# A selective-scan kernel: one 1024-column scan a state in two double-bank PSUM tiles, and all rows of C by DMA

## The chip, the cores and the metric

One core of a Trainium2 chip runs the whole program. Five engines work side by side, each with its own queue in order: TensorE (PE, with its weight loads PEld), VectorE (DVE), ScalarE (ACT), GpSimd (POOL) and SyncE (SP), which here only issues DMAs. The metric is the device time of one execution in microseconds. The time before is the median of three runs.

## The reference

The input x has 16 sequences of 256 steps and 256 features, with a condition vector for each sequence. Four blocks follow one another: a conditioned low-rank adapter, a bidirectional selective state-space layer (Mamba) with a gated MLP, an attention block with 16 heads of 64, and an attention block with 16 heads of 16. Nearly all the time goes into the scan of the second block. Cut to that:

```python
xz = h @ in_w;  xs, z = split(xz);  xs = silu(xs)
proj = xs @ xproj_w                      # 512 + 64 + 64 columns
dt = softplus(proj[..., :512] + dt_bias);  Bm, Cm = the next 64, the last 64
A = -exp(A_log)                          # 512 x 64
def step(hst, (dt_t, B_t, C_t, x_t)):
    hst = hst * exp(dt_t[:, :, None] * A) + (dt_t * x_t)[:, :, None] * B_t[:, None, :]
    y_t = einsum('bds,bs->bd', hst, C_t)
y = ys + xs * Dskip
return y * silu(z) @ out_w
```

It is done once forward in time and once on the sequence reversed, with weights of its own, and the two results are added into x through a gate. There are 64 states, 512 channels and 256 steps, in fp32.

## The kernel before, in words

Channels lie on partitions: 512 channels are 4 chunks (`IC`) of 128 partitions, each with 256 columns of time. A unit is one sequence in one direction; there are 32 units, `units[u] = (b, d)`, and each has 64 states (`NS`). The list `steps` holds all 2048 pairs of unit and state, and the main loop goes over it one state at a time. For a state the work runs through four engines:

- `drive(k)` on POOL (L931): h = dt*x times the row of B of this state, 128 x 1024. The rows of B come as broadcasts from DRAM, four states to a tile `bb` (`load_b`, L901). `drive` runs four states ahead of the scan.
- `decay(k)` on ACT (L946): exp(dt * A) for the state, one activation for each of the four chunks, into PSUM. The tiles `decays` hold half a state each (two chunks, 512 columns, one PSUM bank), and there are `ND` = 3 of them in rotation. Column 0 of each half chunk was set to zero once (L270), so that a scan over two chunks starts anew at the second; the activations write columns 1 to 255 alone. In the backward direction they read time backward.
- `scan(k)` on DVE (L974): two scans of 512 columns, each h = decay * h + input along time, in place in `h`. In the backward direction h is read and written from its end.
- The product with C, in place in `h`: for states with `s % 8` in 0, 2, 3, 5, 6 on DVE (L977), with C from a PSUM tile `cs`, for 1, 4, 7 on POOL (L981), with C from a DRAM broadcast `cb` that holds three rows for eight states (`load_c`, L907). `cs` is made by `spread` (L961): TensorE transposes a column of `cT`, repeated 128 times, into one of two halves of a PSUM bank. So 1280 states have a multiply on DVE and 768 on POOL.
- `add_up(k)` on PE (L992): eight transposes that add into `y` in PSUM, two states behind the scan. An `h` buffer comes free after it; there are 11 (`NH`).

`front(u)` prepares a unit (projections, softplus, the row matrices of B and C written to DRAM as `bd`), `back(u)` applies the output projection, and `rest(b)` runs the remaining layers of a sequence that is finished. Both are generators; the main loop takes a step or two of them for each state, so that their TensorE, ACT and DVE work lies between the scans. The order within an engine's queue is set by the framework's scheduler; what stands under `keep_in_program_order` (POOL's work) stays in the order of the source. After the loop the layers of the last sequence run alone in the tail, with the scan's PSUM tiles as additional banks (`alone`).

PSUM has eight banks: three for `decays`, one for `cs`, two for `y`, two for all other products.

Of the kernel before, what the change touches and what calls it, by code (L numbers as in the profile page):

```python
# [15 lines left out]
P = 128  # L16
# [6 lines left out]
NS = 64  # L23
EPS = 1e-5


# [28 lines left out]
def kernel(ctx: ExitStack, tc: tile.TileContext, a: dict, out: bass.AP):  # L55
# [68 lines left out]
    SG = 4  # L124
    ND = 3
    NH = 11
# [7 lines left out]
    ps_y = ctx.enter_context(tc.tile_pool(name="ps_y", bufs=1, space=PSUM))  # L134
    ps_c = ctx.enter_context(tc.tile_pool(name="ps_c", bufs=1, space=PSUM))
    ps_g = ctx.enter_context(tc.tile_pool(name="ps_g", bufs=2, space=PSUM))
# [119 lines left out]
    for d in ("fwd", "bwd"):  # L256
        an = res.tile([P, IC, NS], F32, name=f"a_neg_{d}")
        nc.sync.dma_start(an, a[f"L1_cond_{d}_A_log"].rearrange("(c p) s -> p c s", p=P))
        nc.scalar.activation(an, an, AF.Exp)
        nc.vector.tensor_scalar(an, an, -1.0, None, ALU.mult)  # L260
        a_neg.append(an)
        w_bc.append(res.tile([P, IC, 2 * NS], F32, name=f"w_bc_{d}"))
        nc.sync.dma_start(w_bc[-1], chunked(a[f"L1_cond_{d}_xproj_w"])[:, :, DI:])
        w_out.append(res.tile([P, IC, D], F32, name=f"w_out_{d}"))
        nc.sync.dma_start(w_out[-1], chunked(a[f"L1_cond_{d}_out_w"]))


    decays = [ps_y.tile([P, 2, T], F32, name=f"decay{j}") for j in range(ND)]
    for dc in decays:
        nc.vector.memset(dc[:, :, 0:1], 0.0)  # L270

# [101 lines left out]
    def front(u):  # L373
# [13 lines left out]
        w_in, w_dt = wfront.pop(u)  # L387
        xz = s2.tile([P, 2 * IC, T], F32, name="xz")
        for m in range(0, 2 * IC, 2):
            px = halves(bank1("pxz"))  # L390
            for j in range(2):
                for c in range(DC):
                    nc.tensor.matmul(  # L393
                        px[:, j], w_in[:, c, (m + j) * P : (m + j + 1) * P], hT[:, c],
                        start=(c == 0), stop=(c == DC - 1),
                    )
                yield
            nc.scalar.copy(xz[:, m : m + 2], px)
        nc.scalar.activation(xz, xz, AF.Silu)
        exp_table()  # L400
        yield
        pb = bank1("pbc")
        for c in range(IC):
            nc.tensor.matmul(pb[:, :T], w_bc[d][:, c], xz[:, c], start=(c == 0), stop=(c == IC - 1))
        bc = s1.tile([P, T], F32, name="bc", tag="uu")
# [3 lines left out]
        yield  # L409
        pt = bank1("pct")  # L410
        for t in range(NT):
            nc.tensor.transpose(pt[:, t * P : (t + 1) * P], bc[:, t * P : (t + 1) * P], ident)
        cT = s2.tile([P, NT, NS], F32, name="cT")
        nc.scalar.copy(cT, pt[:, :T].rearrange("p (t s) -> p t s", t=NT)[:, :, NS:])
        yield


        pr = s1.tile([P, IC, T], F32, name="pr")
        for m in range(0, IC, 2):
            pp = halves(bank1("pdt"))  # L420
            for j in range(2):
                for c in range(IC):
                    nc.tensor.matmul(  # L423
                        pp[:, j], w_dt[:, c, (m + j) * P : (m + j + 1) * P], xz[:, c],
                        start=(c == 0), stop=(c == IC - 1),
                    )
                yield
# [32 lines left out]
        yield  # L460
        tc.keep_in_program_order(nc.gpsimd.tensor_tensor(dtx, dt, xz[:, 0:IC], ALU.mult))  # L461
        st[u] = (xz, cT, bd, dt, dtx)
        yield

    def back(u, yg):
# [12 lines left out]
        for m in range(DC):  # L478
            xb = xs[b][:, m]
            nc.vector.scalar_tensor_tensor(  # L480
                xb, po[:, m], m_mamba[:, 4 + m, b : b + 1], xb, ALU.mult, ALU.add
            )
# [409 lines left out]

    bbs, cbs, ys, made, hs, skips = {}, {}, {}, {}, {}, {}
    cs = ps_c.tile([P, 2, T], F32, name="cs")
    steps = [(u, s) for u in range(len(units)) for s in range(NS)]
    turn = [0]

# [6 lines left out]
    def load_c(u, g):  # L904
        bd = st[u][2]
        cb = s3.tile([P, 3, T], F32, name="cb")
        nc.sync.dma_start(  # L907
            cb,
            bd[NS + 8 * g + 1 : NS + 8 * g + 8 : 3, :].partition_broadcast(P),
        )  # L910
        cbs[u, g] = cb

    def drive(k):
        u, s = steps[k]
        if s % SG == 0:
# [19 lines left out]
    def decay(k):  # L935
        u, s = steps[k]
        d = units[u][1]

        when = slice(1, T) if d == 0 else slice(T - 2, None, -1)
        made[k] = []  # L940
        for i in range(2):
            dc = decays[turn[0] % ND]
            turn[0] += 1
            for j in range(2):
                c = 2 * i + (j if d == 0 else 1 - j)
                nc.scalar.activation(  # L946
                    dc[:, j, 1:T], st[u][3][:, c, when], AF.Exp, scale=a_neg[d][:, c, s : s + 1]
                )
            made[k].append(dc)


    near = [k for k, (u, s) in enumerate(steps) if s % 8 in (0, 2, 3, 5, 6)]
    nth = {k: i for i, k in enumerate(near)}

    def spread(i):

        if i >= len(near):
            return
        u, s = steps[near[i]]
        for t in range(NT):  # L960
            nc.tensor.transpose(  # L961
                cs[:, i % 2, t * P : (t + 1) * P], st[u][1][:, t, s : s + 1].to_broadcast([P, P]), ident
            )

    def scan(k):
        u, s = steps[k]
        d = units[u][1]
        h = hs[k]
        for i, dc in enumerate(made.pop(k)):
            hv = h[:, 2 * i : 2 * i + 2].rearrange("p c t -> p (c t)")  # L970
            dv = dc.rearrange("p c t -> p (c t)")
            if d == 1:
                hv = hv[:, ::-1]
            nc.vector.tensor_tensor_scan(hv, dv, hv, 0.0, ALU.mult, ALU.add)  # L974
        if k in nth:
            c = cs[:, nth[k] % 2]
            nc.vector.tensor_tensor(h, h, c.unsqueeze(1).to_broadcast([P, IC, T]), ALU.mult)  # L977
        else:
            c = cbs[u, s // 8][:, (s % 8) // 3]
            tc.keep_in_program_order(  # L980
                nc.gpsimd.tensor_tensor(h, h, c.unsqueeze(1).to_broadcast([P, IC, T]), ALU.mult)  # L981
            )

    def add_up(k):
# [4 lines left out]
        for n, h in enumerate(([skips.pop(u)] if s == 0 else []) + [hs.pop(k)]):  # L989
            for t in range(NT):  # L990
                for c in range(IC):
# [5 lines left out]
                    )  # L997

# [142 lines left out]
    decay(0)  # L1141
    spread(0)
    spread(1)
    other = late()
    for k in range(len(steps) + BEHIND):
# [9 lines left out]
        if k >= BEHIND:  # L1155
            add_up(k - BEHIND)
        if k - 1 in nth:
            spread(nth[k - 1] + 2)
        if k >= BEHIND:
            u, s = steps[k - BEHIND]  # L1160
            if s == NS - 1:
# [5 lines left out]
                for i in range(2):  # L1167
                    py = halves(bank1("py"))
                    for j in range(2):
# [3 lines left out]
                    nc.vector.tensor_tensor(  # L1173
                        yg[:, 2 * i : 2 * i + 2], py, st[u][0][:, IC + 2 * i : IC + 2 * i + 2], ALU.mult
                    )
# [39 lines left out]
```

## Time and profile before

| what | value |
|---|---|
| median of three runs | 7624.67 us (7620.87 to 7626.77) |
| the profiled execution, first to last instruction (span) | 7616.3 us |
| median of the runs less this span | 8.4 us |
| mean granted TensorE clock | 0.932 |
| DMA, mean | 89 GB/s, 675.90 MB |

The profile is one execution of its own; its page gives the span, and no other time for it. For each group of instructions it gives the source line, engine, operation, the tiles written and read, shape, count, then busy time in us and the mean duration of one in ns, then the idle time of the engine just before these instructions, with what ended most of it. Durations of neighbours on one engine overlap at the ends, so that start-to-start distances are shorter than a row's mean. A wait row says which engine and line waited for which, with the sum, the number of times and the longest, in us. A timeline row gives the start, the length, the engine, the line and how many instructions were merged.

### The profile page before, as it was taken

How to read it: one execution, taken by the hardware profiler on the slowest of the kernel's cores; microseconds unless marked ns; L12 is line 12 of the kernel's file. 1: busy time of each engine (PE TensorE's matmuls, PEld its weight loads, DVE VectorE, ACT ScalarE, POOL GpSimd, SP SyncE). 2: the span in 40 equal slices, each digit the busy share in tenths (PEclk: the TensorE clock that was granted, in tenths of full speed). 3: DMA queues.
4: the chain of work that ended last, by engine and by line, in shares of the span. 5: the costliest groups of instructions: out<-in, count | busy, mean ns of one | idle time of the engine just before them, and what ended most of it. 6: DMA issues, size and time to landing. Idle time of an engine off the chain costs nothing.

```text
span 7616.3 us, 100847 instructions
## 1 busy us (share of the span) xinstructions
PE 6249.2 (82%) x35471; PEld 4952.4 (65%) x35471; DVE 6860.6 (90%) x6887; ACT 5431.2 (71%) x12141; POOL 6843.8 (90%) x2959
## 2 busy tenths in 40 slices
PE   7568888888888888888888888888888888888778
PEld 4456676666667666676666666666666766666655
DVE  3988999999999999999999999999999999999982
ACT  4567777777777777777777777777777777777753
POOL 3999999999999999999999999999999999999960
PEclk8679999999999999999999999999999999999999
DMA  4112232222322222232222223222232222322221
GB/s 166 54 65 92 89 102 76 87 92 88 103 85 93 80 91 95 92 103 73 88 92 91 100 86 98 78 92 93 87 106 79 94 84 89 101 91 89 73 68 49
DMA packets 331644, 675.90 MB, mean 89 GB/s; under 512 B 24724, under 2 KB 204032, under 8 KB 326784
## 3 DMA queue, kind: packets, MB, share of 16 engines
q1 hardware_dynamic: 331136, 669.44, 26.7%
q8 instruction: 280, 4.59, 0.2%
q14 instruction: 228, 1.87, 0.1%
HBM read 650.22 MB, written 10.75 MB: 87 GB/s over the span
## 4 chain that ended last, share of the span: by engine, by line
DVE 47%; POOL 15%; issue 14%; ACT 12%; PE 10%; DVEq 0%; POOLq 0%; ACTq 0%
DVE h L974 34%; POOL h L931 8%; DVE h L977 8%; ACT decay L946 5%; POOL h L981 5%; PE y L992 3%; DVE maxima L682 1%; ACT L155 1%; PE dense L500 1%; PE down L511 1%; PE bank L108 1%; PE po L605 1%; POOL uu L452 1%; POOL dt L458 1%; POOL dtx L461 1%
## 5 line engine op out<-in xcount | busy, mean ns | idle before, releaser
L974 DVE TENSOR_TENSOR_SCAN h<-decay,h 128x512 f32<-128x512 f32 x4096 | 4748.8, 1213 | 283.1 <-ACT decay L946 196.6
L931 POOL TENSOR_TENSOR h<-dtx,bb 128x1024 f32<-128x1024 f32 x2048 | 4793.5, 2367 | 129.2 <-PE y L992 128.4
L992 PE MATMUL y<-ident,h 128*128 128x128 f32 x16384 | 2385.3, 292 | 693.0 <-POOL h L981 639.1
L992 PEld LDWEIGHTS y<-ident,h 128*128 128x128 f32 x16384 | 2054.6, 151 | 1047.6 <-POOL h L981 733.1
L946 ACT ACTIVATE decay<-dt,a_neg_bwd 128x255 f32<-128x255 f32 x4096 | 1816.8, 471 | 759.9 <-DVE h L974 718.3
L946 ACT ACTIVATE decay<-dt,a_neg_fwd 128x255 f32<-128x255 f32 x4096 | 1824.6, 474 | 613.0 <-DVE h L974 571.6
L981 POOL TENSOR_TENSOR h<-h,cb 128x1024 f32<-128x1024 f32 x768 | 1813.2, 2361 | 289.8 <-DVE h L974 275.1
L977 DVE TENSOR_TENSOR h<-h,cs 128x1024 f32<-128x1024 f32 x1280 | 1533.5, 1215 | 66.2 <-PE cs L961 56.6
L961 PE MATMUL cs<-ident,cT 128*128 128x128 f32 x2560 | 521.6, 294 | 131.8 <-DVE h L977 130.3
L961 PEld LDWEIGHTS cs<-ident,cT 128*128 128x128 f32 x2560 | 331.4, 147 | 216.0 <-DVE h L977 192.0
L572 PE MATMUL sc<-k,q 64*128 64x256 f32 x960 | 293.4, 429 | 16.7 <-ACT ex L581 16.0
L393 PE MATMUL pxz<-hTm,w_in 128*128 128x256 f32 x1024 | 267.6, 388 | 15.9 <-DVE maxima L682 12.1
L679 PE MATMUL sc<-kd,qk 128*128 128x512 f32 x490 | 251.4, 614 | 33.5 <-DVE maxima L682 20.8
L700 PE MATMUL scT<-qk,kd 128*128 128x256 f32 x984 | 251.1, 386 | 28.7 <-DVE qk L691 23.2
L581 ACT ACTIVATE ex<-sc,nmax 128x256 f32<-128x256 f32 x480 | 222.7, 468 | 71.2 <-DVE nmax L577 68.5
L423 PE MATMUL pdt<-xz,w_dt 128*128 128x256 f32 x1024 | 247.3, 385 | 0.0
L572 PEld LDWEIGHTS sc<-k,q 64*128 64x128 f32 x960 | 172.6, 200 | 105.3 <-issue 34.2
L393 PEld LDWEIGHTS pxz<-hTm,w_in 128*128 128x128 f32 x1024 | 181.4, 194 | 53.1 <-DVE maxima L682 15.5
L700 PEld LDWEIGHTS scT<-qk,kd 128*128 128x128 f32 x984 | 175.5, 190 | 60.7 <-ACT pr L429 25.0
L577 DVE TENSOR_REDUCE nmax<-sc 128x2 f32<-128x512 f32 x240 | 163.9, 683 | 49.5 <-PE sc L572 48.8
L423 PEld LDWEIGHTS pdt<-xz,w_dt 128*128 128x128 f32 x1024 | 190.7, 194 | 22.2
L595 ACT COPY exT<-pt 128x512 f32<-128x512 f32 x240 | 140.0, 583 | 86.2 <-PE pt L591 84.0
(350 smaller groups left out, 7571.4 us busy)
## 6 DMA issues: line engine op xcount, KB each, us to landing
bb<-bd SPq DMA_DIRECT2D x512, 512.0 KB
cb<-bd SPq DMA_DIRECT2D x256, 384.0 KB
l2w<-in_L_cond_W_dram SPq DMA_DIRECT2D x32, 1024.0 KB
l3w<-in_L_cond_W_dram SPq DMA_DIRECT2D x32, 1024.0 KB
l1w<-in_L_cond_mlp_w_dram SPq DMA_DIRECT2D x48, 512.0 KB
w_in<-in_L_cond_fwd_in_w_dram SPq DMA_DIRECT2D x16, 1024.0 KB
w_dt<-_L_cond_fwd_xproj_w_dram SPq DMA_DIRECT2D x16, 1024.0 KB
w_in<-in_L_cond_bwd_in_w_dram SPq DMA_DIRECT2D x16, 1024.0 KB
```

What stands on the lines that cost most here:

```text
L393: nc.tensor.matmul(px[:, j], w_in[:, c, (m + j) * P : (m + j + 1) * P], hT[:, c], start=(c == 0), stop=(c == DC - 1),)
L423: nc.tensor.matmul(pp[:, j], w_dt[:, c, (m + j) * P : (m + j + 1) * P], xz[:, c], start=(c == 0), stop=(c == IC - 1),)
L572: nc.tensor.matmul(sc[:, t], q[base : base + 64, ch, t * P : (t + 1) * P], k[base : base + 64, ch], start=True, stop=True,)
L679: nc.tensor.matmul(sc, q[:, g, t * P : (t + 1) * P], kd[g % 2][:, 2 * i : 2 * i + 2], start=True, stop=True)
L700: nc.tensor.matmul(sc[:, kt], kd[g % 2][:, j, kt * P : (kt + 1) * P], q[:, g], start=True, stop=True)
L931: nc.gpsimd.tensor_tensor(h, st[u][4], bb.unsqueeze(1).to_broadcast([P, IC, T]), ALU.mult)
L946: nc.scalar.activation(dc[:, j, 1:T], st[u][3][:, c, when], AF.Exp, scale=a_neg[d][:, c, s : s + 1])
L961: nc.tensor.transpose(cs[:, i % 2, t * P : (t + 1) * P], st[u][1][:, t, s : s + 1].to_broadcast([P, P]), ident)
L974: nc.vector.tensor_tensor_scan(hv, dv, hv, 0.0, ALU.mult, ALU.add)
L977: nc.vector.tensor_tensor(h, h, c.unsqueeze(1).to_broadcast([P, IC, T]), ALU.mult)
L981: nc.gpsimd.tensor_tensor(h, h, c.unsqueeze(1).to_broadcast([P, IC, T]), ALU.mult)
L992: nc.tensor.matmul(ys[u][:, t, c * P : (c + 1) * P], h[:, c, t * P : (t + 1) * P], ident, start=(s == 0 and n == 0 and c == 0), stop=(s == ...
```

## The change: what it does

- `decays` becomes two tiles of a whole state each (four chunks, 1024 columns, two banks). The bank of `cs` goes.
- A state has one scan of 1024 columns. For the 1280 states with the product on DVE it writes in place into the decay tile in PSUM, and the multiply reads it there and writes `h`; for the others the scan writes `h`.
- The reset at the start of each chunk no longer comes from a zeroed column: after `front` has used dt, POOL sets its column 0 to 1e34 (`APART`), and A is kept at or below -1e-30, so that the decay there is exp of a very negative number, zero. The activations write all 256 columns.
- All rows of C come by DMA: `cb` holds four states, and one load is made for every four states. `spread`, `cT` and the two transposes that made it go.
- The backward unit is held in reversed time from the projections on: the copies out of PSUM in `front` reverse it, and `back` reverses the result when it is added. Scan and decays have no reversed form any more.
- `xz` becomes two tiles, `xv` (one buffer) and `zv` (two), each with a Silu of its own.

```diff
-    ND = 3
+    ND = 2
...
-        nc.vector.tensor_scalar(an, an, -1.0, None, ALU.mult)
+        nc.vector.tensor_scalar(an, an, -1.0, LEAST, ALU.mult, ALU.min)
...
-    decays = [ps_y.tile([P, 2, T], F32, name=f"decay{j}") for j in range(ND)]
-    for dc in decays:
-        nc.vector.memset(dc[:, :, 0:1], 0.0)
+    decays = [ps_y.tile([P, IC, T], F32, name=f"decay{j}") for j in range(ND)]
...
-            nc.scalar.copy(xz[:, m : m + 2], px)
-        nc.scalar.activation(xz, xz, AF.Silu)
+            to = (xv, zv)[m // IC][:, m % IC : m % IC + 2]
+            nc.scalar.copy(to, px[:, :, ::-1] if d else px)
+        for v in (xv, zv):
+            nc.scalar.activation(v, v, AF.Silu)
...
-        pt = bank1("pct")
-        for t in range(NT):
-            nc.tensor.transpose(pt[:, t * P : (t + 1) * P], bc[:, t * P : (t + 1) * P], ident)
-        cT = s2.tile([P, NT, NS], F32, name="cT")
-        nc.scalar.copy(cT, pt[:, :T].rearrange("p (t s) -> p t s", t=NT)[:, :, NS:])
...
-        tc.keep_in_program_order(nc.gpsimd.tensor_tensor(dtx, dt, xz[:, 0:IC], ALU.mult))
+        tc.keep_in_program_order(nc.gpsimd.tensor_tensor(dtx, dt, xv, ALU.mult))
+        tc.keep_in_program_order(nc.gpsimd.memset(dt[:, :, 0:1], APART))
...
-        cb = s3.tile([P, 3, T], F32, name="cb")
-        nc.sync.dma_start(
-            cb,
-            bd[NS + 8 * g + 1 : NS + 8 * g + 8 : 3, :].partition_broadcast(P),
-        )
+        cb = s3.tile([P, SG, T], F32, name="cb")
+        nc.sync.dma_start(cb, bd[NS + g * SG : NS + (g + 1) * SG, :].partition_broadcast(P))
...
-            if s % 8 == 0:
-                load_c(u, s // 8)
+            load_c(u, s // SG)
...
-        when = slice(1, T) if d == 0 else slice(T - 2, None, -1)
-        made[k] = []
-        for i in range(2):
-            dc = decays[turn[0] % ND]
-            turn[0] += 1
-            for j in range(2):
-                c = 2 * i + (j if d == 0 else 1 - j)
-                nc.scalar.activation(
-                    dc[:, j, 1:T], st[u][3][:, c, when], AF.Exp, scale=a_neg[d][:, c, s : s + 1]
-                )
-            made[k].append(dc)
+        dc = decays[k % ND]
+        for c in range(IC):
+            nc.scalar.activation(dc[:, c], st[u][3][:, c], AF.Exp, scale=a_neg[d][:, c, s : s + 1])
...
-        for i, dc in enumerate(made.pop(k)):
-            hv = h[:, 2 * i : 2 * i + 2].rearrange("p c t -> p (c t)")
-            dv = dc.rearrange("p c t -> p (c t)")
-            if d == 1:
-                hv = hv[:, ::-1]
-            nc.vector.tensor_tensor_scan(hv, dv, hv, 0.0, ALU.mult, ALU.add)
-        if k in nth:
-            c = cs[:, nth[k] % 2]
-            nc.vector.tensor_tensor(h, h, c.unsqueeze(1).to_broadcast([P, IC, T]), ALU.mult)
+        h, dc = hs[k], decays[k % ND]
+        c = cbs[u, s // SG][:, s % SG].unsqueeze(1).to_broadcast([P, IC, T])
+        if s % 8 in (0, 2, 3, 5, 6):
+            nc.vector.tensor_tensor_scan(flat(dc), flat(dc), flat(h), 0.0, ALU.mult, ALU.add)
+            nc.vector.tensor_tensor(h, dc, c, ALU.mult)
         else:
-            c = cbs[u, s // 8][:, (s % 8) // 3]
-            tc.keep_in_program_order(
-                nc.gpsimd.tensor_tensor(h, h, c.unsqueeze(1).to_broadcast([P, IC, T]), ALU.mult)
-            )
+            nc.vector.tensor_tensor_scan(flat(h), flat(dc), flat(h), 0.0, ALU.mult, ALU.add)
+            tc.keep_in_program_order(nc.gpsimd.tensor_tensor(h, h, c, ALU.mult))
...
-    alone += [None] + [t.rearrange("p c t -> p (c t)") for t in (decays[0], cs, decays[1])]
-    alone += [None, decays[2].rearrange("p c t -> p (c t)")]
+    for dc in decays:
+        alone += [None] + [flat(dc[:, i : i + 2]) for i in (0, 2)]
```

More of the change, by code (lines that the diff above doesn't have):

```diff
@@ L24 @@
 EPS = 1e-5
+APART, LEAST = 1e34, -1e-30
 COLUMNS = [
@@ L134 @@
     ps_y = ctx.enter_context(tc.tile_pool(name="ps_y", bufs=1, space=PSUM))
-    ps_c = ctx.enter_context(tc.tile_pool(name="ps_c", bufs=1, space=PSUM))
     ps_g = ctx.enter_context(tc.tile_pool(name="ps_g", bufs=2, space=PSUM))
@@ L387, in front @@
         w_in, w_dt = wfront.pop(u)
-        xz = s2.tile([P, 2 * IC, T], F32, name="xz")
+        xv = s1.tile([P, IC, T], F32, name="xv")
+        zv = s2.tile([P, IC, T], F32, name="zv")
         for m in range(0, 2 * IC, 2):
@@ L403, in front @@
         for c in range(IC):
-            nc.tensor.matmul(pb[:, :T], w_bc[d][:, c], xz[:, c], start=(c == 0), stop=(c == IC - 1))
+            nc.tensor.matmul(pb[:, :T], w_bc[d][:, c], xv[:, c], start=(c == 0), stop=(c == IC - 1))
         bc = s1.tile([P, T], F32, name="bc", tag="uu")
@@ L408, in front @@
         nc.sync.dma_start(bd, bc)
-        yield
-        pt = bank1("pct")
-        for t in range(NT):
-            nc.tensor.transpose(pt[:, t * P : (t + 1) * P], bc[:, t * P : (t + 1) * P], ident)
-        cT = s2.tile([P, NT, NS], F32, name="cT")
-        nc.scalar.copy(cT, pt[:, :T].rearrange("p (t s) -> p t s", t=NT)[:, :, NS:])
         yield
@@ L423, in front @@
                     nc.tensor.matmul(
-                        pp[:, j], w_dt[:, c, (m + j) * P : (m + j + 1) * P], xz[:, c],
+                        pp[:, j], w_dt[:, c, (m + j) * P : (m + j + 1) * P], xv[:, c],
                         start=(c == 0), stop=(c == IC - 1),
@@ L460, in front @@
         yield
-        tc.keep_in_program_order(nc.gpsimd.tensor_tensor(dtx, dt, xz[:, 0:IC], ALU.mult))
-        st[u] = (xz, cT, bd, dt, dtx)
+        tc.keep_in_program_order(nc.gpsimd.tensor_tensor(dtx, dt, xv, ALU.mult))
+        tc.keep_in_program_order(nc.gpsimd.memset(dt[:, :, 0:1], APART))
+        st[u] = (xv, zv, bd, dt, dtx)
         yield
@@ L480, in back @@
             nc.vector.scalar_tensor_tensor(
-                xb, po[:, m], m_mamba[:, 4 + m, b : b + 1], xb, ALU.mult, ALU.add
+                xb, po[:, m, ::-1] if d else po[:, m], m_mamba[:, 4 + m, b : b + 1], xb, ALU.mult, ALU.add
             )
@@ L890, in beside @@
             yield from front(following)
-    bbs, cbs, ys, made, hs, skips = {}, {}, {}, {}, {}, {}
-    cs = ps_c.tile([P, 2, T], F32, name="cs")
+    bbs, cbs, ys, hs, skips = {}, {}, {}, {}, {}
     steps = [(u, s) for u in range(len(units)) for s in range(NS)]
-    turn = [0]
     def load_b(u, g):
@@ L937, in decay, with flat @@
         d = units[u][1]
-        when = slice(1, T) if d == 0 else slice(T - 2, None, -1)
-        made[k] = []
-        for i in range(2):
-            dc = decays[turn[0] % ND]
-            turn[0] += 1
-            for j in range(2):
-                c = 2 * i + (j if d == 0 else 1 - j)
-                nc.scalar.activation(
-                    dc[:, j, 1:T], st[u][3][:, c, when], AF.Exp, scale=a_neg[d][:, c, s : s + 1]
-                )
-            made[k].append(dc)
[L952 to L962, printed above, removed]
-            )
+        dc = decays[k % ND]
+        for c in range(IC):
+            nc.scalar.activation(dc[:, c], st[u][3][:, c], AF.Exp, scale=a_neg[d][:, c, s : s + 1])
+    def flat(t):
+        return t.rearrange("p c t -> p (c t)")
     def scan(k):
         u, s = steps[k]
-        d = units[u][1]
-        h = hs[k]
-        for i, dc in enumerate(made.pop(k)):
-            hv = h[:, 2 * i : 2 * i + 2].rearrange("p c t -> p (c t)")
-            dv = dc.rearrange("p c t -> p (c t)")
-            if d == 1:
-                hv = hv[:, ::-1]
-            nc.vector.tensor_tensor_scan(hv, dv, hv, 0.0, ALU.mult, ALU.add)
-        if k in nth:
-            c = cs[:, nth[k] % 2]
-            nc.vector.tensor_tensor(h, h, c.unsqueeze(1).to_broadcast([P, IC, T]), ALU.mult)
-        else:
-            c = cbs[u, s // 8][:, (s % 8) // 3]
-            tc.keep_in_program_order(
-                nc.gpsimd.tensor_tensor(h, h, c.unsqueeze(1).to_broadcast([P, IC, T]), ALU.mult)
-            )
+        h, dc = hs[k], decays[k % ND]
[3 more added lines that the diff above has]
+            nc.vector.tensor_tensor(h, dc, c, ALU.mult)
+        else:
+            nc.vector.tensor_tensor_scan(flat(h), flat(dc), flat(h), 0.0, ALU.mult, ALU.add)
+            tc.keep_in_program_order(nc.gpsimd.tensor_tensor(h, h, c, ALU.mult))
     def add_up(k):
@@ L1141 @@
     decay(0)
-    spread(0)
-    spread(1)
     other = late()
@@ L1156 @@
             add_up(k - BEHIND)
-        if k - 1 in nth:
-            spread(nth[k - 1] + 2)
         if k >= BEHIND:
@@ L1173 @@
                     nc.vector.tensor_tensor(
-                        yg[:, 2 * i : 2 * i + 2], py, st[u][0][:, IC + 2 * i : IC + 2 * i + 2], ALU.mult
+                        yg[:, 2 * i : 2 * i + 2], py, st[u][1][:, 2 * i : 2 * i + 2], ALU.mult
                     )
```

## The prediction

> **What bounds the kernel now.** I read the page's busy line first, then a table by stretches to cut off head and tail, then the costliest groups, the waits, and a timeline.
>
> ```profile
> PE 6249.2 (82%) x35471; PEld 4952.4 (65%) x35471; DVE 6860.6 (90%) x6887; ACT 5431.2 (71%) x12141; POOL 6843.8 (90%) x2959
> ```
>
> ```profile
> 200.00:7400.00 7200.00, 5929.44 (x34077) 4729.97 (x34075) 6730.44 (x6703) 5271.31 (x11824) 6772.51 (x2915) 0.94 0.27 88
> ```
>
> The second row is the scan loop (length, then PE, PEld, DVE, ACT, POOL busy, clock, DMA share, GB/s). In 7200 us DVE is idle 470 and POOL 427: two engines bound it together, each at 94%. ACT is busy 5271, so it looks free.
>
> ```profile
> L974 DVE TENSOR_TENSOR_SCAN h<-decay,h 128x512 f32<-128x512 f32 x4096 | 4748.8, 1213 | 283.1 <-ACT decay L946 196.6
> L931 POOL TENSOR_TENSOR h<-dtx,bb 128x1024 f32<-128x1024 f32 x2048 | 4793.5, 2367 | 129.2 <-PE y L992 128.4
> L946 ACT ACTIVATE decay<-dt,a_neg_bwd 128x255 f32<-128x255 f32 x4096 | 1816.8, 471 | 759.9 <-DVE h L974 718.3
> L981 POOL TENSOR_TENSOR h<-h,cb 128x1024 f32<-128x1024 f32 x768 | 1813.2, 2361 | 289.8 <-DVE h L974 275.1
> L977 DVE TENSOR_TENSOR h<-h,cs 128x1024 f32<-128x1024 f32 x1280 | 1533.5, 1215 | 66.2 <-PE cs L961 56.6
> ```
>
> ```profile
> ACT decay L946 <- DVE h L974: 1289.9, 1443, 6.2
> DVE h L974 <- ACT decay L946: 196.6, 199, 3.2
> DVE h L974 <- POOL h L931: 80.7, 50, 5.9
> DVE h L977 <- PE cs L961: 56.6, 57, 3.5
> ```
>
> To see here: ACT mostly waits for DVE to give a decay tile back (1289.9), and DVE seldom for ACT (196.6). The three half-state tiles are what keeps it so.
>
> ```profile
> 3016.65 0.88 ACT L946 ACTIVATE decay<-dt,a_neg_fwd 128x255 f32<-128x255 f32 x2 [0.19 <-DVE h L974]
> 3017.65 1.20 DVE L977 TENSOR_TENSOR h<-h,cs 128x1024 f32<-128x1024 f32 x1
> 3018.62 0.59 ACT L595 COPY exT<-pt 128x512 f32<-128x512 f32 x1 [1.09 <-PE pt L591]
> 3019.11 0.88 ACT L946 ACTIVATE decay<-dt,a_neg_fwd 128x255 f32<-128x255 f32 x2
> 3019.36 3.44 DVE L974 TENSOR_TENSOR_SCAN h<-decay,h 128x512 f32<-128x512 f32 x3
> 3019.92 0.46 ACT L581 ACTIVATE ex<-sc,nmax 128x256 f32<-128x256 f32 x1
> ...
> 3020.82 2.18 ACT L946 ACTIVATE decay<-dt,a_neg_fwd 128x255 f32<-128x255 f32 x5
> ```
>
> Three scans take 3.44, so they start (3.44-1.21)/2 = 1.115 us apart although each row says 1.21: the rest overlaps. Other ACT work (copies, exponentials of the layers) stands between decays and holds them up; ACT may run about a state ahead, and so DVE does not feel it.
>
> **Part 1, one scan for two (saves 117).** A 1024-column multiply on DVE is 1.215, a 512-column one 0.685 (L103): 0.530 per 512 columns, 0.155 fixed. The scan is 1.213 for 512, so 1.058 + 0.155, two passes' worth. The fixed 0.155 is only partly seen: 1.115 - 1.058 = 0.057 remains at back-to-back starts. 2048 x 0.057 = 117 us. Ends: 0 (if a 1024-column scan into PSUM pays it again) and 2048 x 0.155 = 317.
>
> The Trainium skill ("Perfetto Trace Analysis", Optimizing Scalar/DVE Operations) gives DVE a per-instruction access overhead of about 60 ns on SBUF and 125 on PSUM; with 125 this part would be 256 us, an estimate. The same section says that grouping helps an engine that is saturated, and that instructions of an engine that is not, but holds up others, are better broken up; it gives no figure for that side. DVE is the first kind here and ACT the second, and the change makes the unit of both twice as large.
>
> **Part 2, the multiply right behind its own scan (costs 111).** In the trace's instruction list, a multiply starts 1.31 after the start of its own 512-column scan (median of 122 such pairs), but 1.115 after another state's: waiting for its input costs 0.19. In the built order of the new kernel 706 of 1280 multiplies stand directly behind their own scan, 122 before: 584 x 0.19 = 111 us. Ends: 0 and, if reading back from PSUM takes twice as long, 222.
>
> [...]
>
> **Part 3, the C transposes go (saves 57).** 2560 transposes (521.6 us of PE, 331.4 of PEld) leave, and with them DVE's 56.6 us of waiting. PE is not the bound; that ACT gets its inputs a little sooner (it waits 378 us for four PE results: po 134.9, bank 86.2, pt 84.0, pxz 73.2) I put at 8% of that, PE's share removed: 30 us saved. Ends 0 and 100.
>
> **Part 4, two whole-state tiles (costs 366).** Now the decays of state k+1 can start when the last reader of state k-1 is done, and all four must be ready before the scan of k+1. From release to scan: 0.03 + 1.80 (four decays in a row in the timeline) + 0.03 = 1.86; the two 0.03 are the smallest distances in the instruction list. In that time DVE does what stands between in its order:
> - k multiplied on POOL (3 in 8): one scan, 1.115 + 1.058 = 2.17. Slack 0.31.
> - k multiplied on DVE: 2.17 + 0.19 + 1.115 = 3.48. Slack 1.62.
> Before, a half tile came back three scans earlier: two scans, 2.23, for 0.03 + 0.92 + 0.03, slack at least 1.25.
>
> The new order has other ACT instructions between the first and the last decay of 1072 states, 1.04 us each on average by rows such as ex 0.46 and exT 0.58. Those cannot run while the first decay waits for its tile. I take for each state 1.86 plus what stands inside, less the DVE work of its window by the same rows, where positive:
> - windows of one scan: 186 of 767 too short, 187 us
> - 118 windows where the order is scan, scan, multiply, multiply, so that both tiles are held and only about 1.29 us of DVE work is left: 129 us
> - 135 others: 55 us
> Together 371. The same count over the order of before gives 5, so its 196.6 us of waits come from lateness that this count does not see (results of PE that ACT waits for); they stay. 371 - 5 = 366. Ends: 0, if the lateness of DVE for other reasons covers all of it, and twice that, since those 196.6 will grow with less slack.
>
> **Part 5, what takes up some of it (saves 81).** DVE's waits for POOL's h (80.7) vanish if DVE is the later one. POOL's own work stays: 6772.5 busy plus 128.4 waiting for h buffers gives 6901 in the loop, 299 under the 7200. That is the floor of any gain.
>
> **Nothing for the rest.** C rows: 512 loads of 512 KB for 256 of 384 KB on SP's queue, +164 MB, DMA share 27% to about 34%. A load starts when the multiply five states back is done and is needed four states later, some 14 us; POOL and DVE show no wait for a C or B row now. SP's queue holds B loads and weights behind each C load that waits; if that cover went, 1 us per load is 512 us. Fronts: 32 pairs of transposes and 32 cT copies of 0.255 go, one 2048 Silu of 1.916 becomes two of about 1.06, and 32 small POOL memsets come (0.1, the nearest rows; at most 0.95): under 10 us, beside other work. The reversed reads replace reversed ones (bwd decays 471 ns, fwd 474). The tail keeps six rotating places.
>
> **Sum.** -117 + 111 - 57 - 30 + 366 - 81 = +192. On the span of 7616.3 that is 7808; the median of the runs lies 8.4 above that span, so **7817**.
>
> **Rivals.**
> - *Faster: ACT's work hides.* If DVE's windows are in fact longer, since POOL makes it wait anyway, part 4 is 0 and part 5 too: -117 + 111 - 57 - 30 = -93, 7532; without part 2's cost 7421. For it: ACT is idle 1929 us in the loop. Against: this idleness lies where ACT waits for tiles, and those come back later. It decides if less than about 93 us of part 4 shows. 0.23.
> - *The C loads come late* on SP's in-order queue: +512; alone 7616.3 + 512 + 8.4 = 8137. Against: 14 us of cover. It shows as POOL or DVE multiplies waiting for a DMA. 0.04.
> - *It cancels:* part 4 at about 90, within 0.2% of 7624.67 (15 us, about what can be measured here). 0.05.
> - *A scan into PSUM runs slower* than one into SBUF; no row shows it. 0.1 us on 1280 scans would be 128 us more; it lies inside the forecast's case.
>
> **Numbers.** The forecast's case, DVE held by ACT at two tiles, has 0.68: 7640 to 8020, where 8020 takes a good half more of part 4. The range reaches into the faster case, to 7560. Slower 0.72, same 0.05, faster 0.23.
>
> **What would show it.** Right: scan groups of 2048 with about 2.27 us; DVE's wait for ACT decay at 400 to 700 us instead of 197; POOL's multiply waiting longer for DVE (275 now); POOL busy unchanged at about 6845; DVE busy about 100 to 250 lower. Wrong: DVE's wait for decays under 250; a DMA wait in front of a multiply; POOL idle falling well under 400 in the loop.

## The result, and the profile after

| | before | after |
|---|---|---|
| median of the runs | 7623.38 us (7620.87 to 7626.77) | 8469.42 us (8466.72 to 8481.77) |
| the profiled execution's span | 7616.3 us | 8467.8 us |
| mean granted TensorE clock | 0.932 | 0.877 |
| DVE / POOL idle in the loop | 470 / 427 of 7200 us | 1267 / 1233 of 8000 us |

The ratio is 1.1111 (95%: 1.1095 to 1.1126): 846 us slower. The prediction said 192 slower, with a range that ends at +395. The side was right, the size was less than a quarter of it.

The page's busy line of the changed kernel, then its row of the table by stretches for the loop (length, then PE, PEld, DVE, ACT, POOL busy, clock, DMA share, GB/s):

```profile
PE 6431.4 (76%) x32847; PEld 4910.4 (58%) x32847; DVE 6881.9 (81%) x4836; ACT 5628.7 (66%) x12203; POOL 6840.7 (81%) x2991
```

```profile
200.00:8200.00 8000.00, 6083.30 (x31383) 4671.97 (x31384) 6732.55 (x4652) 5462.57 (x11877) 6767.27 (x2945) 0.88 0.30 100
```

DVE and POOL are busy as long as before (6860.6 and 6843.8 then). On these two nothing became more expensive; some 800 us of idle time came to each. (ACT is busy 198 us longer, 5628.7 for 5431.2, with 2839 us idle.) So it is a wait, and the groups say which:

```profile
L940 DVE TENSOR_TENSOR_SCAN decay<-decay,h 128x1024 f32<-128x1024 f32 x1280 | 2918.9, 2289 | 681.6 <-ACT decay L930 457.4
L944 POOL TENSOR_TENSOR h<-h,cb 128x1024 f32<-128x1024 f32 x768 | 1805.3, 2351 | 1263.1 <-DVE h L943 1195.6
L930 ACT ACTIVATE decay<-dt,a_neg_bwd 128x256 f32<-128x256 f32 x4096 | 1880.6, 472 | 892.6 <-DVE h L941 600.7
L943 DVE TENSOR_TENSOR_SCAN h<-decay,h 128x1024 f32<-128x1024 f32 x768 | 1753.2, 2283 | 319.5 <-ACT decay L930 304.7
L941 DVE TENSOR_TENSOR h<-decay,cb 128x1024 f32<-128x1024 f32 x1280 | 1549.3, 1219 | 28.0 <-PE pv L769 0.4
```

The waits of the changed kernel (sum, times, longest):

```profile
ACT decay L930 <- DVE h L941: 1215.9, 719, 8.8
POOL h L944 <- DVE h L943: 1195.6, 512, 11.6
PE y L954 <- POOL h L944: 1146.4, 484, 6.7
DVE decay L940 <- ACT decay L930: 457.4, 284, 14.8
ACT decay L930 <- DVE h L943: 446.2, 551, 4.4
DVE h L943 <- ACT decay L930: 304.7, 188, 4.8
DVE decay L940 <- issue: 141.6, 183, 3.3
DVE decay L940 <- POOL h L921: 78.9, 28, 4.9
```

DVE waits for decays 457.4 + 304.7 = 762 us, against 197. A row that names "issue" is a wait for which no releaser was found; its 141.6 us in front of scans belong here too, since in nearly every one of these cases a decay ends 0.08 to 0.10 us before the scan starts. That makes 904. Sums below are of the rows that name ACT, with the "issue" rows added where they matter. ACT in turn waits 1215.9 + 446.2 for DVE to give tiles back. Each waits for the other, as in a ring of buffers that is too short. Its lateness goes on in order: POOL's multiply waits for DVE 1195.6 (275 before), PE's transposes for POOL 1146.4 (639).

One stretch of the timeline of the changed kernel (start, length, engine, line), some of DVE's rows first, then ACT's:

```profile
3011.07 1.22 DVE L941 TENSOR_TENSOR h<-decay,cb 128x1024 f32<-128x1024 f32 x1
3012.21 0.41 DVE L687 TENSOR_TENSOR qk<-qk,pm 128x256 f32<-128x256 f32 x1
3012.53 2.28 DVE L943 TENSOR_TENSOR_SCAN h<-decay,h 128x1024 f32<-128x1024 f32 x1
3014.73 1.26 DVE L678 TENSOR_REDUCE maxima<-sc 128x2 f32<-128x512 f32 x2
3019.26 2.30 DVE L940 TENSOR_TENSOR_SCAN decay<-decay,h 128x1024 f32<-128x1024 f32 x1 [3.26 <-issue]
```

```profile
3008.43 2.01 ACT L930 ACTIVATE decay<-dt,a_neg_bwd 128x256 f32<-128x256 f32 x4 [1.38 <-DVE h L943]
3010.38 0.58 ACT L399 COPY zv<-pxz 128x512 f32<-128x512 f32 x1
3010.97 1.28 ACT L401 ACT_TABLE_LOAD   x1
3012.26 1.06 ACT L401 ACTIVATE zv<-zv 128x1024 f32<-128x1024 f32 x1
3013.34 1.28 ACT L156 ACT_TABLE_LOAD   x1
3014.64 0.48 ACT L930 ACTIVATE decay<-dt,a_neg_bwd 128x256 f32<-128x256 f32 x1
3016.62 0.60 ACT L699 ACTIVATE ex<-scT 128x512 f32<-128x512 f32 x1 [1.51 <-PE scT L696]
3017.12 2.05 ACT L930 ACTIVATE decay<-dt,a_neg_bwd 128x256 f32<-128x256 f32 x5
```

The multiply gives a tile back at 3012.29. ACT is then in 4.2 us of work of a `front`, makes one decay, and waits 1.51 for a PE result of a layer, with the other decays queued behind. The run of decays ends at 3019.17, the scan starts at 3019.26, and DVE has stood 3.26 us (the row names no engine as releaser; a decay ends 0.09 us before the scan starts). One finished state in the other tile, a scan of some 2.2 us, is all that covers a refill of four decays. Before, two finished half tiles covered about as much (2.23 in the prediction), but a refill was only two decays. Note also the 2.01 for four decays in an undisturbed row; the prediction took 1.80.

### The profile page after: what moved, and what is told of

Read it like the earlier page. It is cut to its first block, busy times and chain, and to the rows that moved or that the text cites. A ratio compares the mean times of both kernels' runs of the same rounds, so it can differ in the third digit from the quotient of the medians.

```text
span 8467.8 us, 93639 instructions
## 1 busy us (share of the span) xinstructions
PE 6431.4 (76%) x32847; PEld 4910.4 (58%) x32847; DVE 6881.9 (81%) x4836; ACT 5628.7 (66%) x12203; POOL 6840.7 (81%) x2991
## 5 line engine op out<-in xcount | busy, mean ns | idle before, releaser
L954 PE MATMUL y<-ident,h 128*128 128x128 f32 x16384 | 2604.1, 311 | 1418.7 <-POOL h L944 1146.4
L940 DVE TENSOR_TENSOR_SCAN decay<-decay,h 128x1024 f32<-128x1024 f32 x1280 | 2918.9, 2289 | 681.6 <-ACT decay L930 457.4
L954 PEld LDWEIGHTS y<-ident,h 128*128 128x128 f32 x16384 | 2200.3, 161 | 1977.0 <-POOL h L944 1326.3
L944 POOL TENSOR_TENSOR h<-h,cb 128x1024 f32<-128x1024 f32 x768 | 1805.3, 2351 | 1263.1 <-DVE h L943 1195.6
L930 ACT ACTIVATE decay<-dt,a_neg_bwd 128x256 f32<-128x256 f32 x4096 | 1880.6, 472 | 892.6 <-DVE h L941 600.7
L930 ACT ACTIVATE decay<-dt,a_neg_fwd 128x256 f32<-128x256 f32 x4096 | 1868.0, 472 | 876.5 <-DVE h L941 615.2
L943 DVE TENSOR_TENSOR_SCAN h<-decay,h 128x1024 f32<-128x1024 f32 x768 | 1753.2, 2283 | 319.5 <-ACT decay L930 304.7
L941 DVE TENSOR_TENSOR h<-decay,cb 128x1024 f32<-128x1024 f32 x1280 | 1549.3, 1219 | 28.0 <-PE pv L769 0.4
L418 PE MATMUL pdt<-xv,w_dt 128*128 128x256 f32 x1024 | 254.9, 391 | 3.1 <-ACT bc L408 0.2
L699 ACT ACTIVATE ex<-scT 128x512 f32<-128x512 f32 x246 | 144.4, 587 | 108.3 <-PE scT L696 107.3
L418 PEld LDWEIGHTS pdt<-xv,w_dt 128*128 128x128 f32 x1024 | 191.4, 195 | 32.8 <-ACT q L755 5.5
```

What stands on the lines that cost most here:

```text
L418: nc.tensor.matmul(pp[:, j], w_dt[:, c, (m + j) * P : (m + j + 1) * P], xv[:, c], start=(c == 0), stop=(c == IC - 1),)
L930: nc.scalar.activation(dc[:, c], st[u][3][:, c], AF.Exp, scale=a_neg[d][:, c, s : s + 1])
L940: nc.vector.tensor_tensor_scan(flat(dc), flat(dc), flat(h), 0.0, ALU.mult, ALU.add)
L941: nc.vector.tensor_tensor(h, dc, c, ALU.mult)
L943: nc.vector.tensor_tensor_scan(flat(h), flat(dc), flat(h), 0.0, ALU.mult, ALU.add)
L944: tc.keep_in_program_order(nc.gpsimd.tensor_tensor(h, h, c, ALU.mult))
```

## The experiments

Times are device us; "before" is a run of the kernel before beside the version. Most versions ran once, and I read nothing into differences under some 20 us: the kernel before itself lay between 7618 and 7633. The edits are shortened to the lines that matter.

**1. Which part: half tiles again.** All of the change stays, but a state has two half tiles, out of four, each with a scan and a multiply of 512 columns.

```diff
-    ND = 2                                       # tiles of [P, IC, T]
+    ND = 4                                       # tiles of [P, 2, T]
+    dc = decays[(2 * k + c // 2) % ND]           # scan, scan, multiply, multiply by halves
```

> The new kernel, but the four PSUM banks of the decays are four tiles of half a state: two scans of 512 columns and, on DVE, two multiplies of 512 columns from PSUM; C still comes by DMA for every state, time is still reversed. Theory A (two whole-state tiles leave ACT no room, so DVE waits for decays): DVE's wait for decays falls from 762 us to under 350 and the time to 7600 to 7900, though two scans and two multiplies cost some 190 us more of DVE. Rival B (C by DMA, or scans that write PSUM, are the cost): above 8300. Rival C (any kernel whose multiply waits for its own scan loses this much): above 8300 too.

Measured: 7789.1 (before 7633.3). 680 of the 846 us come back.

```profile
DVE decay L942 <- ACT decay L930: 183.2, 135, 5.8
DVE h L949 <- ACT decay L930: 113.8, 74, 2.4
```

DVE's wait for decays falls from 762 to 297. C by DMA, scans into PSUM, reversed time and the new Silus are all still in. None of them makes most of the loss.

**2. Is it ACT's four activations?** One activation makes a whole state's decays, first on the two whole-state tiles, then two of 512 columns make them on the four half tiles. Both versions leave out the other chunks' own factors: an activation takes the factor of its first chunk.

```diff
-        for c in range(IC):
-            nc.scalar.activation(dc[:, c], st[u][3][:, c], AF.Exp, scale=a_neg[d][:, c, s : s + 1])
+        nc.scalar.activation(flat(dc), flat(st[u][3]), AF.Exp, scale=a_neg[d][:, 0, s : s + 1])
```

> The new kernel, but one activation of 1024 columns for each state in place of four of 256, with the first chunk's A for all four: it leaves out the other chunks' own factors. ACT needs about 1.1 us from release to scan instead of 1.86. Theory A: the slack of a window with one scan rises from 0.3 to 1.05 us; DVE's wait for decays falls under 300, time 7350 to 7750. Rival B: nothing in it changes, above 8300. Rival D (ACT is late because it waits in its queue for results of TensorE, not because of its own work): about half of the loss stays, 7950 to 8250.

> Four half-state tiles as in e1_half_tiles, and one activation of 512 columns for each half with its first chunk's A (it leaves out the other chunk's own factor): ACT's work falls as in e2_one_decay, which with whole-state tiles still took 8002 us. If the whole-state tile as such costs time even when ACT is quick: 7550 to 7750. If e2 stayed high because quick decays only move the wait to another engine: 7900 or more.

Measured: 8001.9 (before 7633.3) on whole tiles, 7639.9 (before 7630.4) on halves. With quick ACT the whole tile still costs 362 us. The first run fell between my theories. Its waits of DVE:

```profile
DVE decay L939 <- POOL h L921: 371.0, 149, 13.8
DVE decay L939 <- ACT decay L929: 200.0, 69, 6.0
DVE h L942 <- POOL h L921: 147.2, 107, 3.1
```

The decays now hold DVE 209 us, all groups together, but POOL's h holds it 371.0 + 147.2. The wait moved along the loop.

**3. The ring alone, in the kernel before.** Only the number of half tiles is changed, three to two.

```diff
-    ND = 3
+    ND = 2
```

> The kernel before with two half-state tiles in rotation in place of three; nothing else of the change. The bank that comes free is used in the tail alone. Theory A: a half tile comes back two scans earlier, so that 0.98 us of ring stands against one scan of 1.115: slack 0.13 us in the worst windows, like the new kernel's 0.1 to 0.3. DVE's wait for decays rises from 197 to 600 us or more, time 8100 to 8500. If the loss belongs to wide scans, chained decays or the C rows alone: 7650 to 7850.

Measured: 8140.0 (before 7630.4): 510 slower, with no other part of the change in it.

```profile
DVE h L975 <- ACT decay L947: 729.4, 483, 6.9
```

It is a wait of the same kind and about as long as in the changed kernel (762, or 904 with "issue"; no such row here). What the two share is not the number of columns in PSUM, 1024 here and 2048 there, but the slack: by the expectation above 1.115 - 0.98 = 0.13 us here, and 0.14 in the changed kernel (worked out below). The granted clock is 0.925 here, near the 0.932 of before, so that the 0.877 of the changed kernel is not needed for a loss of this size.

**4. The order of release alone.** Half tiles as in experiment 1, with DVE's scans and ACT's decays held in a written order. In one kernel DVE takes the halves in the order in which ACT fills them, in the other the other way round, so that the half that ACT needs first comes back last.

```diff
-            for i in (0, 1):                     # straight
+            for i in (1, 0):                     # crossed
```

> The control for e12_half_crossed: the same holding of decays and scans, with scans first half, second half. Theory A: 7750 to 7950, near e1_half_tiles. If holding the order of the decays costs by itself, this run rises with e12_half_crossed.

> e1_half_tiles (7789 us) with the decays held in the order of the chunks and the scans of a state in the order second half, first half. No instruction is added. A state's first scan then needs all four decays, and the tile that ACT fills first comes back last, as with one tile for a whole state. Theory A: most of the loss comes back, 8200 to 8500. If the loss lies in the chain of four activations that wait for one another in one tile: 7750 to 7950.

Measured: 7894.9 straight, 8288.4 crossed: 393 us for the order in which equal work gives back equal tiles. First two rows straight, the others crossed:

```profile
DVE decay L953 <- ACT decay L941: 202.7, 124, 3.2
DVE h L960 <- ACT decay L941: 136.5, 88, 3.3
```

```profile
DVE decay L953 <- issue: 259.3, 138, 4.8
DVE decay L953 <- ACT decay L941: 183.0, 70, 7.5
DVE h L960 <- ACT decay L941: 123.8, 70, 3.3
```

The straight kernel is 106 slower than experiment 1, which has no written order. Both fell where the theory of the ring had put them; a loss by the chain of activations alone would have left them equal.

**5. Earlier release, or other covers, on the whole tile.** Four attempts to loosen it without more PSUM: the multiply in two halves; the scan in two halves; the transposes three states behind instead of two; all of ACT in source order.

```diff
+            for i in (0, 2): nc.vector.tensor_tensor(h[:, i:i+2], dc[:, i:i+2], c[:, i:i+2], ALU.mult)   # product
+            for i in (0, 2): nc.vector.tensor_tensor_scan(...)  # scan, 512 columns each
-    AHEAD, BEHIND = 4, 2
+    AHEAD, BEHIND = 4, 3
+        tc.keep_in_program_order(nc.scalar.activation(...))     # every ACT instruction
```

> The new kernel with the DVE multiply in two of 512 columns, one for each bank of the decay tile; the scan stays one of 1024 columns. The first bank comes back 0.6 us earlier, the second as before. If late release of the tile is what counts: 8150 to 8350. If the need counts (all four decays before the scan may start): 8400 to 8550, as two more instructions cost DVE some 70 us.

> The new kernel with two scans of 512 columns, one for each bank, and one multiply of 1024. A scan may start when two decays are there, and behind the scans of states multiplied on POOL each bank comes back by itself. If the need counts: 7850 to 8150, near the run with half tiles, although 117 us of DVE time come back. If only the release behind the multiply counts: 8400 to 8600.

> The new kernel with the transposes that add up y three states behind the scan in place of two, so that TensorE reaches a state's h later and stands less in front of POOL's multiply. If TensorE waiting in its queue for POOL's multiply (1146 us), and with it every layer product that ACT and DVE wait for behind it, is what makes ACT late: TensorE's wait falls under 500 us and the time to 7900 to 8200. If ACT is late from its own work and its tiles alone: 8350 to 8500, with TensorE's wait gone but DVE's wait for decays still near 760.

> The new kernel, but all ACT instructions stay in the order of the source, so that the four decays of a state stand together and other work stands between states. Part 4 of the prediction (other work inside a group of decays costs 366 us): DVE's wait for decays falls by 300 or so, time 8050 to 8200. If where the other work stands makes no difference, because it stands ahead of the next group then: 8400 to 8550. If work in the order of the source waits longer for TensorE: above 8600.

Measured: 8632.4, 8898.8, 8714.6, 8676.2, all slower than the change itself; only the last lies in a range that had been named. The whole tile is the unit of dependence: splitting the reader gives nothing back earlier (with two multiplies ACT starts on the tile only after the second, in all 734 cases in which it waits; with two scans the second waits for the first in the same tile, some 1.26 start to start against 1.13). With the transposes further behind, PE's wait for POOL is 1205 (1146 in the changed kernel) and DVE's decay wait 736 (762). So this edit did not take away the wait that it was made to take away, and it does not test whether PE's wait is what makes ACT late: that theory stays open. With ACT in source order the decay wait is 569, but in the loop DVE then waits 617 for results of PE, against 226 in the changed kernel. The transposes three states behind, in the kernel before:

> The kernel before with the transposes three states behind the scan. Its TensorE waits 639 us for POOL's multiply. If that wait holds up the layers' work and through ACT the scans, 7450 to 7590; if nothing hangs on it 7600 to 7650; if h buffers come free too late for POOL (128 us waited now), 7650 to 7800.

Measured: 7690.3, ratio 1.0084 (1.0067 to 1.0101). This is in the last of the three ranges, though POOL's wait for h buffers rose by only 34 us (128.4 to 162.5).

**6. The scan into PSUM.** The scan always writes `h` in SBUF, so that the decay tile is free after it, and the multiply reads `h`.

```diff
-            nc.vector.tensor_tensor_scan(flat(dc), flat(dc), flat(h), 0.0, ALU.mult, ALU.add)
-            nc.vector.tensor_tensor(h, dc, c, ALU.mult)
+            nc.vector.tensor_tensor_scan(flat(h), flat(dc), flat(h), 0.0, ALU.mult, ALU.add)
+            nc.vector.tensor_tensor(h, h, c, ALU.mult)
```

> The new kernel, but every scan writes h in SBUF, and DVE multiplies h by the row of C with both inputs in SBUF. A decay tile is free after its scan, not after the multiply. Theory A: windows behind a DVE multiply lose nothing and tiles come back 1.2 us earlier, which alone brings 100 to 300 us: 8150 to 8350. Against it, if DVE and POOL get in each other's way with two SBUF inputs, multiplies on DVE or POOL's rows get longer than 1.22 and 2.36 us, and the time goes above 8600.

Measured: 9410.0.

```profile
L941 DVE TENSOR_TENSOR h<-h,cb 128x1024 f32<-128x1024 f32 x1280 | 3150.2, 2464 | 23.5
L921 POOL TENSOR_TENSOR h<-dtx,bb 128x1024 f32<-128x1024 f32 x2048 | 5574.9, 2747 | 0.1
```

With both inputs in SBUF the multiply takes 2.464 instead of 1.219, and POOL's product 2.747 instead of 2.360. Two SBUF inputs alone do not make the multiply longer: the shortest of the 1280 takes 1.193, the longest 3.446, which is about one product of POOL more. I read that as DVE and POOL waiting for one another; the changed kernel shows none of it. With the C rows in SBUF, the scan into PSUM is what avoids this.

**7. Is it the layers' ACT work?** Both kernels with `rest(b)` cut to its last transposes and the output. (The layers after the scan are left out of both.)

> The kernel before without the layers behind the scan (the function rest keeps only the last transposes and the output): ACT, TensorE and DVE then have the scans and the fronts alone. POOL has all its work, some 6850 us with the head. Theory A: 6950 to 7200, POOL as the bound.

> The new kernel, likewise without the layers. If the ring of two whole-state tiles is too tight by itself (four decays in a chain, 2.07 us against 2.21 of one scan, with some wait between engines not seen): 300 us or more over the kernel before without layers. If it is tight only because the layers' ACT work falls into it, which is what the forecast's part 4 said: within 100 us of it, or faster.

Measured: 7058.2 and 7632.8: still 575 apart. Of before, then of after:

```profile
DVE h L837 <- ACT decay L809: 254.1, 125, 4.2
DVE h L837 <- POOL h L794: 110.0, 74, 5.9
```

```profile
DVE decay L803 <- ACT decay L793: 729.0, 508, 14.8
DVE h L806 <- ACT decay L793: 271.3, 187, 3.8
```

So most of the loss, 575 of 846, is there without the layers' work between the decays, on which I had put most of the price. A quiet stretch of the changed kernel without layers shows what is left:

```profile
3102.10 2.28 DVE L806 TENSOR_TENSOR_SCAN h<-decay,h 128x1024 f32<-128x1024 f32 x1
3105.38 2.30 DVE L803 TENSOR_TENSOR_SCAN decay<-decay,h 128x1024 f32<-128x1024 f32 x1 [1.00 <-ACT decay L793]
```

```profile
3102.22 1.50 ACT L793 ACTIVATE decay<-dt,a_neg_fwd 128x256 f32<-128x256 f32 x3 [1.52 <-DVE h L804]
3104.41 2.29 ACT L793 ACTIVATE decay<-dt,a_neg_fwd 128x256 f32<-128x256 f32 x5 [0.70 <-DVE h L806]
```

ACT has made three of the four decays by 3103.72 and then stands until the scan ends at 3104.38. In the built order, the first decay of the state after next is queued ahead of the fourth. It needs the tile that the scan still holds. Then two activations stand between release and scan, and DVE waits 1.00. In the built order of the full changed kernel 679 of 2048 states have a decay of the next state inside like this.

**8. The decays in their own order.** Each decay is held behind the decay before it, in the changed kernel, in its version without layers, and in the kernel before.

```diff
+    def in_turn(ins): ...                        # an order edge, without a semaphore, to the decay before
-            nc.scalar.activation(dc[:, c], ...)
+            in_turn(nc.scalar.activation(dc[:, c], ...))
```

> The new kernel without the layers (7633 us, against 7058 for the kernel before without them), with the decays held in their order; 924 states are crossed without that. Theory E: 6950 to 7150, POOL as the bound again. If the ring is too tight by itself: 7400 or more.

> The new kernel with its decays held in their own order, state after state; all other ACT work stays free to move. In the new kernel's built order the first decay of the next state stands ahead of the last decay of the current one in 679 of 2048 states, and there waits for the scan in between; the run without layers shows the next scan 1.07 us late behind it. Theory E (this crossing is the greater part of the loss): 679 times 1.07 is 727 us, less what the wait hid, so 7700 to 8000. If the ring of two tiles is too tight whatever the order: 8300 or more. If other work moves in between instead: 8000 to 8300.

> The kernel before with its decays held in their order, where now the first decay of the next half tile stands ahead of the last of the current one in 1253 of 4096 cases. With three tiles that has a scan more of room, and DVE waits 197 us in all. If these waits come from the crossing: 7480 to 7600, faster than the kernel before. If not, or if chained decays cost as much: 7600 to 7750.

Measured without layers: 7479.6, 153 better, still 421 over before without layers. By the expectation, the ring is too tight by itself. In quiet stretches scans now follow one another at 2.21; what remains sits where ACT work of a `front` or a `back` falls into the ring: in 170 of the 178 waits for decays ACT did work other than decays during the wait or in the 2.2 us before it. In the full kernel: 8487.3, no gain; DVE's wait for decays is 583 (687 with "issue", against 904), but in the loop it waits 428 for results of PE, against 226. My theory that the crossed decays are most of the loss fell. In the kernel before: 7592.8 (7587.1 to 7597.6) against 7621.7, ratio 0.9956 (0.9940 to 0.9973). This is the one version that is faster than the kernel before, by 0.44%. Its time is in the range of the first theory, but not for the reason given there: DVE's wait for decays rose from 196.6 to 266.9. Its wait for POOL's h fell from 81 to 16.

**9. The Silus.** The trace of the changed kernel has table loads of ACT that nobody had asked for: 63 at the Silu line and 31 at the decay line, 32 and none before. The two Silus were scheduled apart, with decays between them. This kernel has one tile and one Silu again.

```diff
-        for v in (xv, zv):
-            nc.scalar.activation(v, v, AF.Silu)
+        nc.scalar.activation(xz, xz, AF.Silu)
```

> The changed kernel with one tile for xs and z again and one Silu of 2048 columns a unit, as before the change. Two separate Silus let the scheduler put decays between them, and then ACT loads its function tables twice more: the trace of the changed kernel has 63 table loads at the Silu line and 31 at the decay line, against 32 and none before, 62 x 1.283 = 80 us of ACT work that the prediction did not count. (To make room, a 128 x 128 selection matrix of the last attention block is left out, and its 64 matmuls become 256 small ones from columns of the identity.) Theory: ACT work that falls into a ring of two tiles is paid in full; then 8469 falls by about 80, and by up to 160 if the lateness is carried on through POOL and PE: 8310 to 8390, DVE's wait for decays 762 falls by 60 to 140. Rival: these loads lie where ACT waits for tiles anyway (it is idle 2800 us); then 8450 to 8480. Other rival: the loads make most of the 846; then below 8100.

Measured: 8671.4 (8670.8 to 8672.8), ratio to before 1.1366 (1.1347 to 1.1385). The loads went (ACT busy 5552.2 instead of 5628.7) and the kernel became 202 slower than the change. All three expectations missed.

```profile
DVE decay L943 <- ACT decay L933: 647.5, 320, 6.1
DVE h L946 <- ACT decay L933: 223.5, 193, 3.8
```

DVE waits 871 for decays (943 with "issue", against 904) with less ACT work. What had changed besides is the scheduler's order, and the small matmuls named above.

## Why the prediction was right or wrong

**Right: the bound, the cause and the side.** DVE and POOL bound the kernel before, the decay tiles hold them after, and experiments 1, 3 and the pair of 2 show that the ring of tiles is enough to cause most of it: 680 us back with half tiles, 510 us lost from two tiles alone, 362 us for the whole tile even with quick ACT.

**Part 1 (117): 104.** Scans of 1024 columns follow one another at 2.207, two of 512 took 2 x 1.129; 2048 x 0.051 = 104. The estimate of 256 from the 125 ns of the Trainium skill ("Perfetto Trace Analysis", Optimizing Scalar/DVE Operations) is not what this trace shows: 51 ns a state.

**Part 2 (111): 85.** A multiply starts 2.327 after the start of its own wide scan, another state's multiply 2.181 after (medians of 705 and 132 pairs): 0.146 and not 0.19. 584 x 0.146 = 85.

**Part 3 (57 + 30): the wait went.** No multiply waits for C now. But DVE's waits for other results of PE in the loop grew from 90 to 226 us, so the 57 were more than lost again. That ACT gained by it can't be seen below 1662 us of waiting for tiles.

**Part 4 (366): the step that failed; it was mis-sized.** It priced DVE's longer wait for decays at 366 us; the wait grew by 707 (197 to 904). Its place was right; three of its terms were not.
- The ring was taken as 0.03 + 1.80 + 0.03 = 1.86. Four activations into one tile take 2.01, because each waits for the one before it: 0.51 start to start, where unchained ones show 0.41. So 2.07, and the slack behind a scan is 2.21 - 2.07 = 0.14, not 0.31.
- Only other ACT work was counted inside a state's decays. The next state's decays were left out, as if they were harmless; the order that I had in hand shows 679 of them, and the timeline of experiment 7 shows one that costs 1.00 us. What they cost in all is not shown: taking them away brought 153 us without the layers and nothing with them.
- Each window was priced as if ACT came into it on time and DVE, POOL and PE stood ready. But a late scan makes POOL's multiply late, the transposes and POOL's next h late, and ACT's own next release later. In the loop, DVE stands in front of a scan behind a POOL state 510 times of 762 (608 us; the count gave 186 windows and 187 us), and behind the others 230 times (370 us; 253 windows and 184 us). That handed-on lateness makes the difference is my reading; the waits fit it, but no experiment takes it alone.

The 707 lie just inside the part's upper end, "twice that", but the forecast's range took only a good half more: with 707 in place of 366 the sum gives 8158, past 8020. On top come the saving of part 5, which did not come, and the waits for PE of part 3: DVE's idle time in the loop grew by 797 in all, 2.2 times the 366.

**Part 5 (81): did not come.** DVE still waits 87 us for POOL's h (81 before). I had set a wait to zero because DVE would be the later one. My reading, not tested: lateness comes in bursts, and then POOL has fallen behind too (idle 427 to 1233 us).

**"Nothing for the rest".** DMA share 30%, not 34%; no multiply waits for a C load, so that rival fell; POOL busy 6840.7 as said, its memsets 0.105. Wrong for the Silus: "one becomes two" also brought 62 table loads of 1.283, 80 us of ACT work inside the ring, as the timeline above shows. Experiment 9 does not show that they cost time.

**The marks.** Scan mean 2.287 (2.27 said), POOL's multiply waiting longer, no DMA wait: as said. DVE's wait for decays, 762 or 904, is over the 400 to 700. "DVE busy 100 to 250 lower" was wrong: it is 21 higher. The sum of the three kinds of rows fell by 61 (4748.8 + 1533.5 to 2918.9 + 1753.2 + 1549.3), but neighbours overlap at their ends, and with more gaps between them I take it that less of that overlap is counted once. DVE's busy time was no mark for this change.

**What stays open.** How the 846 divide among the shorter ring, the crossed decays and `front` work. Each edit that takes one away also gets another order from the scheduler. Six versions with two whole-state tiles and four decays each, all with the layers (experiments 5, 8 and 9), lie between 8487 and 8899; no one edit of that ring brought it back, and the three kernels with half tiles and straight order (experiments 1, 2 and 4) lie between 7640 and 7895.

## What to carry to other kernels

Before merging two buffers into one, work out the time from the last reader's end to the next reader's start with everything that its queue has in between, the next round's own instructions included, and compare it with the shortest work of the reader in that time; in the two rings here a slack of 0.13 or 0.14 us was none. If the difference is near zero, a count window by window is too low, here by about a factor of two for the wait itself: keep the smaller tiles. Where two engines are at 94%, the third that looks 27% idle may be what their buffers depend on.

## What the runs showed of the hardware

- Activations that write different parts of one tile were chained, across its two banks too: the four of a state start 0.51 us apart when the decays are held in turn (experiment 8), each with a wait on ACT's own semaphore. In the straight half-tile kernel of experiment 4 they start 0.50 apart within a tile and 0.41 from one tile to the next. So it is the tile that ties them, and no limit of ACT.
- A DVE multiply with both inputs in SBUF beside a busy POOL: 2.464 us against 1.219 with one input in PSUM, and POOL's product 2.747 against 2.360. The Trainium skill ("SBUF — State Buffer", SBUF: two separate sides) says that a DVE instruction with two SBUF inputs and a GpSimd instruction that reads SBUF share a pair of ports, and that whichever starts first has the pair for its whole length. Here both became slower, DVE by 1.25 us and POOL by 0.39 on the mean, and the spread from 1.193 to 3.446 for one multiply fits waits of up to one POOL product.
- A scan that writes PSUM in place takes what one into SBUF takes: 2.289 and 2.283 us for 1024 columns.
